# Fused graph-attention layers on one core: layer-0 steps ahead of the W_out products, six summed key tiles in place of five, weights prepared inside entry 0

## Chip, cores and metric

The kernel runs on one core of a Trainium2 chip. Times are device microseconds of that core: the median of ten executions, and one execution recorded by the hardware profiler, from which all durations of single instructions come.

## What is computed

Eight batch entries, each with N = 2048 nodes and D = 256 features, go through two attention layers with residual and layer norm after each. `adj` is one 2048 x 2048 matrix for all entries.

```python
# layer 0, for each of 8 heads of 32 features (the prior is adj itself)
x_proj = einsum('bnd,hdf->bhnf', x, W)
e = leaky_relu(e_src[..., :, None] + e_dst[..., None, :], 0.2)
e = e + softplus(beta_tilde) * log(adj + 1e-6)
attn = softmax(where(adj > 0, e, -max))
x1 = layernorm(x + concat_heads(attn @ x_proj) @ W_out.T)
# layer 1, one head
h1, h2, h3 = x1 @ W1, x1 @ W2, x1 @ W3
p = softmax(where(adj > 0, leaky_relu(h1 @ h2.T, 0.2), -1e12))
out = layernorm(x1 + relu(p @ h3))
```

## The kernel before

**Layer 0** is `Gat`. Its attention weights are products of a query row and a key column under a maximum, times a matrix `mt` that depends on `adj` alone; so a tile of scores for one head and 128 keys, `s`, is one VectorE instruction of 128 x 2048 (L304). Heads are taken in four pairs (NP = 4), keys in sixteen tiles (NT = 16). One *step* is one pair and one key tile: 64 steps per entry. A step loads a 1 MB `mt` tile (L180; two buffers), makes two `s` (four buffers, so two steps' worth), and gives them to TensorE in `products` (L329): `val` multiplies them by the projected features, `den` by the row of key factors `e`, spread over 32 columns, which sums the denominators. Both accumulate in PSUM over the sixteen tiles.

For entries 1 to 7, the key tiles in `SUMMED` don't get `den` products. Instead the first of them is scaled into two tiles `d` by ScalarE (L317), each later one is multiplied and added into `d` by VectorE one step later (L311, one instruction per head), and at the last step one `den<-d,ones` product brings the sums into PSUM.

```python
    SUMMED = (1, 4, 7, 10, 13)
```

`finish` ends a pair: ScalarE copies `val` into `ht` and `den` into `dn`; the denominators go through DRAM (`rc` L346, reciprocal L347, `rec_d` L348) and come back spread over rows as `rb` (L354); after every second pair VectorE multiplies `ht` by `rb` (L356). `rb` takes a buffer of the same two as `d`.

**Between the layers** stands what is called the seam here. `output` (L369) multiplies `ht` by the transposed W_out for sixteen row tiles, giving `y`; VectorE adds the residual (L371) and takes statistics, ScalarE normalizes, the rows go to `x1_d` and stay in `h3`. `turn` transposes them into `x1t` (L384) and multiplies by W3 (L389).

**Layer 1** is `Dot`, sixteen row tiles. `queries` gives `h1` (L409, once for four row tiles), `scores` the products `e` (L420), a mask addition with row minimum on VectorE (L425) and Exp on ScalarE (L426); `step` transposes the result (L439, copied by L441) and multiplies it by `h3` into `acc` (L455).

**The order.** TensorE executes in the order in which the program is written; the instructions of the other engines are put in order by a scheduler when the kernel is built, and each engine, SP's DMA queue among them, then works its list through in order. Entry 0's layer 0 is run first, with the projections of entries 1 to 7 (`project`, six pieces per entry: four row groups, then the exponentials with the multiplication of `v`, then the query rows) spread evenly over its 64 steps, and with `make_pen`, which turns `adj` rows into a bf16 mask in DRAM. During its first pair it also makes the sixteen `mt` tiles (`make_mt`: two passes on VectorE, L165 and L168, two on ScalarE, transposes L173, copies L174). After that, seven times, layer 1 of entry b - 1 runs together with the 64 steps of layer 0 of entry b. The last layer 1 runs alone. The places of the steps are written by hand:

```python
        for k, _ in enumerate(gat.output()):
            if k % 4 == 3:
                layer_0(1)
        for k, _ in enumerate(gat.turn()):
            if k % 2 == 1:
                layer_0(1)
        dot = Dot(gat)
        dot.step(lambda k: layer_0((2, 1, 1)[k]))
        for i in range(NT - 2):
            dot.step(lambda k: layer_0((0, 2 - (i % 2 == 1), 2 - (i % 14 == 13))[k]))
```

That is 4 steps in `output`, 8 in `turn`, 52 in the `Dot` phase. The weights W_out, W1 W2 and W3 are prepared before anything else (L121 to L149): loaded, transposed by TensorE, and W1 W2 multiplied out.

Of the kernel before, what the change touches and what calls it, by code (L numbers as in the profile page):

```python
# [9 lines left out]
F32 = mybir.dt.float32  # L10
BF16 = mybir.dt.bfloat16
I32 = mybir.dt.int32
AF = mybir.ActivationFunctionType
ALU = mybir.AluOpType
# [4 lines left out]
P = 128  # L19
# [4 lines left out]
NO_EDGE = -3.0e38  # L24
# [3 lines left out]
def kernel(  # L28
# [26 lines left out]
    nc = tc.nc  # L55
    B, N, D = x.shape
    H, _, DH = w_proj.shape
    NT = N // P
    KC = D // P
    BK = 512  # L60
    NB = N // BK
    HALF = N // 2
    HP = 2
    NP = H // HP
    IG = BK // P
    SUMMED = (1, 4, 7, 10, 13)

    const = ctx.enter_context(tc.tile_pool(name="const", bufs=1))
    dram = ctx.enter_context(tc.tile_pool(name="dram", bufs=1, space=DRAM))
# [7 lines left out]
    def mm_tile(name):  # L77
        return ps.tile([P, BK], F32, tag="mm", name=name)
# [39 lines left out]
            nc.vector.tensor_mul(wa, wp[:, kc, 0:D], a_bc)  # L118
            nc.vector.tensor_reduce(dst[:, kc, :], wa.rearrange("p (h f) -> p h f", h=H), AX.X, ALU.add)

    def load_square(w, name):  # L121
        t = chunk.tile([P, KC, D], F32, tag="ht", name=name, bufs=3)
        nc.sync.dma_start(t, w.rearrange("(k p) c -> p k c", p=P))
        return t

    def transposed_square(src, dst):
        for kc in range(KC):
            t = mm_tile("sq_t")
            for o in range(KC):
                nc.tensor.transpose(t[:, ts(o, P)], src[:, o, ts(kc, P)], ident)  # L130
            nc.scalar.copy(dst[:, kc, :], t[:, 0:D])


    wot = const.tile([P, KC, D], F32)
    transposed_square(load_square(w_out, "wo"), wot)


    w1t = chunk.tile([P, KC, D], F32, tag="ht", name="w1t", bufs=3)
    transposed_square(load_square(w1, "w1s"), w1t)
    w2t = chunk.tile([P, KC, D], F32, tag="ht", name="w2t", bufs=3)  # L140
    transposed_square(load_square(w2, "w2s"), w2t)
    w12 = const.tile([P, KC, D], F32)
    for dc in range(KC):
        t = mm_tile("w12p")
        for kc in range(KC):
            nc.tensor.matmul(t[:, 0:D], w1t[:, kc, ts(dc, P)], w2t[:, kc, :], start=(kc == 0), stop=(kc == KC - 1))
        nc.scalar.copy(w12[:, dc, :], t[:, 0:D])
    w3s = const.tile([P, KC, D], F32)
    nc.sync.dma_start(w3s, w3.rearrange("(k p) d -> p k d", p=P))  # L149


    mt_d = dram.tile([N, N], F32, name="mt_d")
# [30 lines left out]
    def make_pen(it):  # L183
        a = wide_tile("adj_r", "d", 2, I32)
        nc.sync.dma_start(a, adj[ts(it, P), :])
        pen = wide_tile("pen", "pen", 1, BF16)
        nc.vector.tensor_scalar(pen, a, 0.0, NO_EDGE, ALU.is_le, ALU.mult)
        nc.sync.dma_start(pen_d[ts(it, P), :], pen)

    def layer_norm(z):  # L190
# [16 lines left out]
    class Gat:  # L207
# [8 lines left out]
        def project(self):  # L216


            b = self.b
            kept = "v" if b == 0 else ("h3", "x1t")[b % 2]  # L220
            self.v = v = whole.tile([P, NT, D], F32, tag=kept, name="v")
            ed = small.tile([P, NT, H], F32, name="ed", bufs=1)
            es = small.tile([P, H, NT], F32, name="es", bufs=1)
            xb = x[b].rearrange("(t p) d -> p t d", p=P)
            xrs, xts = [], []

            def turn(g):
                if g % 2 == 0:
                    xr = wide.tile([P, 2 * IG, D], F32, tag="p", name="xr", bufs=2)
                    nc.sync.dma_start(xr, xb[:, ts(g // 2, 2 * IG), :])  # L230
                    xrs.append(xr)
                xt = chunk.tile([P, KC, BK], F32, tag="ht", name="xt", bufs=3)
                for kc in range(KC):
                    t = mm_tile("tr")
                    for k in range(IG):
                        nc.tensor.transpose(t[:, ts(k, P)], xrs[-1][:, g % 2 * IG + k, ts(kc, P)], ident)
                    nc.scalar.copy(xt[:, kc, :], t)
                xts.append(xt)

            turn(0)  # L240
            for g in range(NB):
                if g + 1 < NB:
                    turn(g + 1)
                for k in range(IG):
                    it = g * IG + k
                    t = mm_tile("proj")
                    for kc in range(KC):
                        nc.tensor.matmul(t[:, 0:D + 2 * H], xts[g][:, kc, ts(k, P)], wp[:, kc, :],
                                         start=(kc == 0), stop=(kc == KC - 1))
                    nc.scalar.copy(v[:, it, :], t[:, 0:D])  # L250
                    nc.scalar.copy(ed[:, it, :], t[:, D:D + H])
                    nc.scalar.copy(es[:, :, it], t[:, D + H:D + 2 * H])
                yield
            top = small.tile([P, 2, H], F32, name="top", bufs=1)
            nc.vector.tensor_reduce(top[:, 0, :], ed.rearrange("p t h -> p h t"), AX.X, ALU.max)
            nc.gpsimd.partition_all_reduce(top[:, 1, :], top[:, 0, :], P, bass_isa.ReduceOp.max)
            nc.vector.tensor_tensor(es, es, top[:, 1, :].unsqueeze(2).to_broadcast([P, H, NT]), ALU.add)
            nc.vector.tensor_tensor(ed, ed, top[:, 1:2, :].to_broadcast([P, NT, H]), ALU.subtract)
            self.re = re = small.tile([P, 2, NT, H], F32, name="re", bufs=2)
            nc.scalar.activation(re[:, 0], ed, AF.Exp, scale=-(1.0 - ALPHA))  # L260
            nc.scalar.activation(re[:, 1], ed, AF.Exp)
            v4 = v.rearrange("p t (h f) -> p (t h) f", f=DH)
            nc.vector.tensor_tensor(v4, v4, re[:, 1].rearrange("p t h -> p (t h)").unsqueeze(2).to_broadcast(
                [P, NT * H, DH]), ALU.mult)
            if b > 0:
                nc.sync.dma_start(v_d[b], v)
                nc.sync.dma_start(re_d[b], re)
            yield
            t = mm_tile("est")
            nc.tensor.transpose(t[:, 0:P], es.rearrange("p h t -> p (h t)"), ident)  # L270
            est = row_tile("est")[:, 0:P]
            nc.scalar.activation(est, t[:, 0:P], AF.Exp, scale=1.0 - ALPHA)
            nc.sync.dma_start(c_d[b].rearrange("h (t p) -> (h t) p", p=P), est)
            yield
# [13 lines left out]
        def step(self, count=1):  # L288

            for _ in range(count):  # L290
# [14 lines left out]
                    s.append(sa)  # L305
                v, e = self.v, self.re[:, 1]
                heads = [hp * HP + a for a in range(HP)]
                summed = self.b > 0 and jt in SUMMED
                if self.b > 0 and jt - 1 in SUMMED[1:]:
                    for d, sa, h in zip(self.sums, self.last, heads):  # L310
                        nc.vector.scalar_tensor_tensor(d, sa, e[:, jt - 1, h:h + 1], d, ALU.mult, ALU.add)  # L311
                self.last = s
                self.products(self.val, [v[:, jt, ts(h, DH)] for h in heads], s, jt == 0, jt == NT - 1)
                if self.b > 0 and jt == SUMMED[0]:
                    self.sums = [wide_tile("d", "d", 2) for _ in heads]
                    for d, sa, h in zip(self.sums, s, heads):
                        nc.scalar.activation(d, sa, AF.Copy, scale=e[:, jt, h:h + 1])  # L317
                if not summed:
                    self.products(self.den, [e[:, jt, h:h + 1].to_broadcast([P, DH]) for h in heads], s, jt == 0,
                                  self.b == 0 and jt == NT - 1)  # L320
                if self.b > 0 and jt == NT - 1:
                    self.products(self.den, [ones] * HP, self.sums, False, True)
                if jt == NT - 1:
                    self.finish(hp)
# [143 lines left out]
    gats = [Gat(b) for b in range(B)]  # L468
    for _ in gats[0].project():
        pass  # L470
    others = (1 for g in gats[1:] for _ in g.project())
    pieces = (B - 1) * (NB + 2)
    for k in range(NP * NT):
        gats[0].step()
        for _ in range((k + 1) * pieces // (NP * NT) - k * pieces // (NP * NT)):
            next(others)
        if k >= NT and (k - NT) % 3 == 2:
            make_pen((k - NT) // 3)
    for _ in others:
        pass  # L480


    dot = None
    for b in range(1, B + 1):
        gat, fresh = gats[b - 1], gats[b] if b < B else None

        def layer_0(count):
            if fresh:
                fresh.step(count)

        if fresh:
            fresh.load()
        if dot is not None:
            dot.step()
        for k, _ in enumerate(gat.output()):
            if k % 4 == 3:
                layer_0(1)
        for k, _ in enumerate(gat.turn()):
            if k % 2 == 1:
                layer_0(1)  # L500
        dot = Dot(gat)
        dot.step(lambda k: layer_0((2, 1, 1)[k]))
        for i in range(NT - 2):
            dot.step(lambda k: layer_0((0, 2 - (i % 2 == 1), 2 - (i % 14 == 13))[k]))
    dot.step()


# [29 lines left out]
```

## Time and profile before

| | |
|---|---|
| Median of ten executions | 4519.67 us (4515.73 to 4523.06) |
| Profiled execution, and its span | 4517.64 us, 4515.9 us |
| TensorE products busy | 4307.0 us (95%) |
| TensorE weight loads busy | 2226.0 us (49%) |
| VectorE busy | 3530.6 us (78%) |
| ScalarE busy | 1772.0 us (39%) |
| DMA | 852 MB, 189 GB/s on average |

The span runs from the first to the last recorded instruction. A group of the profile is named by the line of the kernel, the engine, the operation and `out<-in`; then come the count, the busy time, the mean of one instruction in ns, and the idle time of the engine just before these instructions with what ended it. PE is TensorE, PEld its weight loads, DVE VectorE, ACT ScalarE, SPq the queue that issues the DMAs. One fp32 product of the program shows as two in the trace, and products overlap: a `val` or a `den` of one step is 16 products of about 0.6 us each, but the next operation starts 1.7 us later.

### The profile page before, as it was taken

To read this page: it belongs to the slowest core of one execution; us is meant where nothing else is said; L and a number is where in the kernel's file an instruction comes from. 1 tells how busy PE (TensorE), PEld (TensorE's weight loads), DVE (VectorE), ACT (ScalarE), POOL (GpSimd) and SP (SyncE) were. 2 spreads that over 40 slices of the span, in tenths; PEclk is the share of its full clock that TensorE was granted. 3 is DMA by queue.
4 is the path that set the end of the run, shared out by engine and by line. 5 is a ranking of instruction groups with operands and counts; after the bars stand their busy time and mean duration, and the time that the engine had idled before them with its cause. 6 is when DMAs were issued, how large, how long until landed. Compare 5 with 4: busy or idle time off the path is not lost.

```text
span 4515.9 us, 61388 instructions
## 1 busy us (share of the span) xinstructions
PE 4307.0 (95%) x25372; PEld 2226.0 (49%) x25372; DVE 3530.6 (78%) x2541; ACT 1772.0 (39%) x3739; POOL 4.5 (0%) x14
## 2 busy tenths in 40 slices
PE   6888889999999999999999999999999999999899
PEld 4433335445445544555445554555454554555566
DVE  5787788887889888887888888887988888888222
ACT  6622233334333343333433343333333343333554
POOL 0000000000000000000000000000000000000000
PEclk9999999999999999999999999999999999999999
DMA  7788864556555464555545565555545565554211
GB/s 219 261 297 323 299 216 173 193 185 211 186 179 190 159 222 172 193 181 209 190 173 177 181 218 176 187 188 194 209 160 187 179 213 187 182 178 142 68 49 40
DMA packets 252777, 852.06 MB, mean 189 GB/s; under 512 B 33616, under 2 KB 152400, under 8 KB 174928
## 3 DMA queue, kind: packets, MB, share of 16 engines
q1 hardware_dynamic: 252496, 848.13, 53.9%
q8 instruction: 199, 3.26, 0.3%
q14 instruction: 82, 0.67, 0.0%
HBM read 772.15 MB, written 75.37 MB: 188 GB/s over the span
## 4 chain that ended last, share of the span: by engine, by line
PE 65%; DVE 11%; issue 5%; DMA 3%; ACT 1%; SPq 0%; DVEq 0%
PE acc L455 17%; PE e L420 16%; PE val L329 13%; PE den L329 10%; DVE s L304 8%; PE pt L439 5%; DVE d L311 2%; PE y L369 2%; PE h1p L409 2%; DMA mt<-mt_d 1%; DMA rb<-rec_d 1%; ACT p L426 1%; DVE p L425 1%; PE h3p L389 0%; DVE ht L356 0%
## 5 line engine op out<-in xcount | busy, mean ns | idle before, releaser
L304 DVE SCALAR_TENSOR_TENSOR s<-c,re,mt 128x2048 f32<-128x2048 f32 x1024 | 2347.7, 2344 | 247.9 <-PE den L329 176.1
L329 PE MATMUL val<-s,v 128*32 128x512 f32 x8192 | 1040.9, 603 | 74.4 <-DVE s L304 74.2
L455 PE MATMUL acc<-h,pts 128*128 128x256 f32 x4096 | 949.9, 380 | 8.3 <-ACT pts L441 8.3
L420 PE MATMUL e<-x1t,h 128*128 128x512 f32 x2048 | 904.7, 594 | 0.0
L455 PEld LDWEIGHTS acc<-h,pts 128*128 128x128 f32 x4096 | 748.2, 190 | 99.2 <-ACT pts L441 13.3
L329 PE MATMUL den<-s,re 128*32 128x512 f32 x5952 | 751.2, 593 | 0.0
L420 PEld LDWEIGHTS e<-x1t,h 128*128 128x128 f32 x2048 | 379.5, 190 | 450.8 <-issue 421.0
L329 PEld LDWEIGHTS val<-s,v 128*32 128x32 f32 x8192 | 239.0, 110 | 696.3 <-issue 508.9
L441 ACT COPY pts<-pt 128x512 f32<-128x512 f32 x512 | 296.9, 583 | 644.7 <-PE pt L439 644.5
L311 DVE SCALAR_TENSOR_TENSOR d<-s,re,d 128x2048 f32<-128x2048 f32 x224 | 518.4, 2345 | 0.0
L422 ACT ACTIVATE p<-e 128x512 f32<-128x512 f32 x512 | 303.5, 596 | 480.4 <-PE e L420 480.4
L425 DVE CUSTOM_DVE_ANT_0 p<-p,pen 128x2048 f32<-128x2048 f32 x128 | 292.9, 2289 | 251.5 <-ACT p L422 251.5
L329 PEld LDWEIGHTS den<-s,re 128*32 128x32 f32 x5952 | 205.7, 110 | 448.8 <-issue 447.9
L426 ACT ACTIVATE p<-p,neg 128x2048 f32<-128x2048 f32 x128 | 256.8, 2006 | 255.1 <-DVE neg L425 255.1
L439 PEld LDWEIGHTS pt<-ident,p 128*128 128x128 f32 x2048 | 238.1, 141 | 228.4 <-issue 166.4
L439 PE MATMUL pt<-ident,p 128*128 128x128 f32 x2048 | 318.7, 279 | 9.9 <-ACT p L426 9.9
L463 DVE TENSOR_TENSOR z<-z,x1r 128x256 f32<-128x256 f32 x128 | 54.1, 423 | 255.7 <-ACT z L462 251.7
L462 ACT ACTIVATE z<-acc,rec 128x256 f32<-128x256 f32 x128 | 60.6, 474 | 352.6 <-PE acc L455 352.6
L369 PE MATMUL y<-wot,ht 128*128 128x256 f32 x512 | 138.9, 427 | 60.2 <-DVE ht L356 60.1
L197 ACT ACTIVATE f<-mv,eps_ln 128x1 f32<-128x1 f32 x256 | 74.4, 290 | 270.8 <-DVE mv L195 270.7
L369 PEld LDWEIGHTS y<-wot,ht 128*128 128x128 f32 x512 | 106.0, 214 | 100.4 <-DVE ht L356 63.4
L389 PE MATMUL h3p<-w3s,x1t 128*128 128x256 f32 x512 | 132.7, 385 | 6.9 <-ACT x1t L385 6.9
(81 smaller groups left out, 2100.9 us busy)
## 6 DMA issues: line engine op xcount, KB each, us to landing
mt<-mt_d SPq DMA_DIRECT2D x496, 1024.0 KB, 4.8
c<-c_d SPq DMA_DIRECT2D x64, 1024.0 KB, 6.4
pen<-pen_d SPq DMA_DIRECT2D x128, 512.0 KB, 3.3
xr<-in_x_dram SPq DMA_DIRECT2D x16, 1024.0 KB, 8.5
adj_t<-in_adj_dram SPq DMA_DIRECT2D x16, 1024.0 KB, 6.9
mt_d<-mt SPq DMA_DIRECT2D x16, 1024.0 KB, 5.6
adj_r<-in_adj_dram SPq DMA_DIRECT2D x16, 1024.0 KB, 8.1
rb<-rec_d SPq DMA_DIRECT2D x64, 256.0 KB, 4.1
```

Source lines behind the costliest of these rows:

```text
L304: nc.vector.scalar_tensor_tensor(sa, self.cs[a], self.re[:, 0, jt, h:h + 1], mt, ALU.max, ALU.mult)
L311: nc.vector.scalar_tensor_tensor(d, sa, e[:, jt - 1, h:h + 1], d, ALU.mult, ALU.add)
L329: nc.tensor.matmul(dst[ts(q, DH), ts(c, BK)], weights[q % 2], s[q % 2][:, ds(q // 2 * HALF + c * BK, BK)], start=start, stop=stop)
L369: nc.tensor.matmul(y[:, 0:D], ht[:, ts(it, P)], wot[:, g, :], start=(g == 0), stop=(g == 1))
L389: nc.tensor.matmul(t[:, 0:D], x1t[:, kc, ts(it - 1, P)], w3s[:, kc, :], start=(kc == 0), stop=(kc == KC - 1))
L420: nc.tensor.matmul(t, self.h1[:, kc, ts(it % IG, P)], self.x1t[:, kc, ts(c, BK)], start=(kc == 0), stop=(kc == KC - 1))
L422: nc.scalar.activation(p[:, ts(c, BK)], t, AF.Prelu, alpha=ALPHA)
L425: nc.vector.tensor_tensor_reduce(p, p, pen, -1.0, FMAX, ALU.add, ALU.min, neg)
L426: nc.scalar.activation(p, p, AF.Exp, bias=neg, scale=-1.0, accum_out=den)
L439: nc.tensor.transpose(t[:, ts(k, P)], p[:, ts(g * IG + k, P)], ident)
L441: nc.scalar.copy(pt, t)
L455: nc.tensor.matmul(acc, now[:, ts(k, P)], self.h3[:, j, :], start=(j == 0), stop=(j == NT - 1))
```

## The change

Four things change together.

- At a seam, four steps of the next entry's layer 0 are issued ahead of the W_out products. `output` then has two steps in place of four, and the `Dot` phase 50 in place of 52.
- `SUMMED` becomes one list per head pair: tiles 1, 2, 3 and 13 for the first pair, and six tiles for each of the other three.
- The preparation of the weights becomes a generator, run inside entry 0 after its fifth and ninth steps. The projections of the later entries start later and less densely during entry 0's first pair; the last three pieces of entry 7's are done after entry 0's last step, ahead of the four steps of the first seam.
- Smaller ones: the mask is made by ScalarE in two passes in place of VectorE in one, and the two small copies of a projection tile become one.

```diff
-    SUMMED = (1, 4, 7, 10, 13)
+    SUMMED = ((1, 2, 3, 13),) + ((1, 3, 6, 8, 11, 13),) * (NP - 1)
...
-    transposed_square(load_square(w_out, "wo"), wot)
...
+    def later_weights():
...
+        transposed_square(load_square(w_out, "wo"), wot)
+        yield
+        squares = []
+        for w in (w1, w2):
+            squares.append(chunk.tile([P, KC, D], F32, tag="ht", name="sq", bufs=3))
+            transposed_square(load_square(w, "ws"), squares[-1])
+        for dc in range(KC):
+            t = mm_tile("w12p")
+            for kc in range(KC):
+                nc.tensor.matmul(t[:, 0:D], squares[0][:, kc, ts(dc, P)], squares[1][:, kc, :],
+                                 start=(kc == 0), stop=(kc == KC - 1))
+            nc.scalar.copy(w12[:, dc, :], t[:, 0:D])
+        nc.sync.dma_start(w3s, w3.rearrange("(k p) d -> p k d", p=P))
+        yield
...
-        nc.vector.tensor_scalar(pen, a, 0.0, NO_EDGE, ALU.is_le, ALU.mult)
+        nc.scalar.activation(pen, a, AF.Relu, bias=1.0, scale=-1.0)
+        nc.scalar.mul(pen, pen, NO_EDGE)
...
-                    nc.scalar.copy(ed[:, it, :], t[:, D:D + H])
-                    nc.scalar.copy(es[:, :, it], t[:, D + H:D + 2 * H])
+                    nc.scalar.copy(both[:, it, :], t[:, D:D + 2 * H])
...
-                summed = self.b > 0 and jt in SUMMED
-                if self.b > 0 and jt - 1 in SUMMED[1:]:
+                chain = SUMMED[hp] if self.b > 0 else ()
+                if jt - 1 in chain[1:]:
...
-    others = (1 for g in gats[1:] for _ in g.project())
-    pieces = (B - 1) * (NB + 2)
+    others = [(1 for g in gats[1:] for _ in g.project())] + [later_weights()]
+    LEFT = 3
+    pieces, made = (B - 1) * (NB + 2) - LEFT, 0
     for k in range(NP * NT):
         gats[0].step()
-        for _ in range((k + 1) * pieces // (NP * NT) - k * pieces // (NP * NT)):
-            next(others)
+        if k in (4, 8):
+            next(others[1])
+
+        due = max(k - 3, 0) * 2 // 5 if k < NT else 5 + (k + 1 - NT) * (pieces - 5) // (NP * NT - NT)
+        while made < due:
+            next(others[0])
+            made += 1
...
         if dot is not None:
             dot.step()
+        for _ in others[0]:
+            pass
+        layer_0(4)
         for k, _ in enumerate(gat.output()):
-            if k % 4 == 3:
+            if k % 8 == 7:
                 layer_0(1)
...
-            dot.step(lambda k: layer_0((0, 2 - (i % 2 == 1), 2 - (i % 14 == 13))[k]))
+            dot.step(lambda k: layer_0((0, 2 - (i % 2 == 1), 2 - (i % 4 == 3))[k]))
```

## Prediction

> **What bounds the kernel now.** I read three views in this order: the page's groups, the waits of TensorE, and the busy times of the stages with the timelines around a seam. The span is 4515.9 us, the execution took 4517.6, the median of the runs is 4519.7: sums below are made against the profiled one and carried over with those 2 us added.
>
> ```profile
> L304 DVE SCALAR_TENSOR_TENSOR s<-c,re,mt 128x2048 f32<-128x2048 f32 x1024 | 2347.7, 2344 | 247.9 <-PE den L329 176.1
> L329 PE MATMUL den<-s,re 128*32 128x512 f32 x5952 | 751.2, 593 | 0.0
> L311 DVE SCALAR_TENSOR_TENSOR d<-s,re,d 128x2048 f32<-128x2048 f32 x224 | 518.4, 2345 | 0.0
> ```
>
> The first row is one score tile for one head: 2.344 us, two per step, 4.69 us. The third is one addition into a denominator sum, 2.345 us. VectorE's idle time before score tiles is mostly waiting for TensorE to free a buffer, so TensorE leads on average.
>
> ```profile
> PE val L329 <- DVE s L304: 74.2, 52, 10.9
> PE y L369 <- DVE ht L356: 60.1, 8, 19.6
> PE mtp L173 <- DVE m L168: 18.0, 5, 6.6
> ...
> PE sq_t L130 <- DMA w2s<-in_L_gnn_W_dram: 7.4, 1, 7.4
> ```
>
> What TensorE waited for: total, times, longest. The y row is the seams: once 19.6 us, then about 5.4 at each of six seams, then 8.6 at the last.
>
> ```profile
> 209.30:556.80 347.50, 303.22 (x2074) 131.57 (x2070) 273.33 (x140) 79.53 (x320) 3.02 (x6) 0.95 0.85 309
> 556.80:660.30 103.50, 78.55 (x485) 38.02 (x482) 84.18 (x81) 35.54 (x117) 0.00 (x0) 0.90 0.62 217
> 660.30:1092.50 432.20, 430.38 (x2531) 219.00 (x2529) 358.70 (x232) 164.25 (x277) 0.00 (x0) 1.00 0.53 186
> 1092.50:1176.00 83.50, 75.43 (x481) 36.55 (x480) 76.15 (x79) 34.71 (x119) 0.00 (x0) 0.98 0.59 198
> ```
>
> Stages (length, then busy PE, PEld, DVE, ACT): entry 0 after its first head pair; first seam up to the first h1p; Dot phase; second seam. In the Dot phase TensorE is full and VectorE 83%. At the seam VectorE is 91% busy, and TensorE's "busy" includes waiting inside products.
>
> ```profile
> 1088.99 0.35 DVE L347 RECIPROCAL rc<-rc 128x32 f32<-128x32 f32 x1 [3.04 <-DMA rc<-dn]
> ...
> 1096.16 2.29 DVE L356 TENSOR_TENSOR ht<-ht,rb 128x2048 f32<-128x2048 f32 x1 [1.81 <-DMA rb<-rec_d]
> ```
> ```profile
> 1091.63 4.63 SPq L465 DMA_DIRECT2D out_dram<-z  x2
> 1096.30 2.15 SPq L365 DMA_DIRECT2D h<-in_x_dram  x4
> 1098.48 0.66 SPq L180 DMA_DIRECT2D mt<-mt_d  x1
> ```
>
> VectorE's and SP's queues at the second seam: ht is ready at 1098.45, and SP stands behind the last output store until 1096.3.
>
> **What the Trainium skill says.** "Perfetto Trace Analysis", per-engine timelines, calls ACT and DVE "strict FIFO": what stands behind ht in VectorE's queue waits with it. The trace agrees: at 1096.16 the queue idles 1.81 us for rb. The same page, identifying the most-contended engine, calls matmul busy time a poor measure; it agrees, since 75.43 us are called busy in a seam whose products take some 68. "VectorE: DVE Perf Modes", the perf-mode tier table, keeps fp32 operations on two tensors at one element per cycle, 2293 ns at 2048; ours take 2344, so an added sum costs the full price.
>
> **The change, part by part.**
>
> *Sums.* The chains go from 4x5 to 4+3x6 = 22 tiles per entry. One tile's den products take 1.72 us (in the timeline a den starts at 1025.79 and what follows it at 1027.50). TensorE loses 2x1.72 = 3.4 us per entry, 24 over seven entries. Additions go from 32 to 36 per entry, 28x2.345 = +66 us for VectorE.
>
> *Dot phase.* It holds 50 steps in place of 52 (two were moved to the seam). TensorE: two val (3.4), and 36 den in place of 40 (6.9): -10.3 us. VectorE: -9.4 for the two steps, +14.1 for three more pairs of additions, 363 of 422 us. Summed per row block, VectorE needs 31.7 against TensorE's 29.7, 29.6 and 27.9 in three of fifteen blocks; two steps of lead cover most of it, and I take 2 us of stalls per phase (0 to 6).
>
> *A seam, before.* From 1092.5 to the first h1p at 1176.0: 83.5 us, of which TensorE's work is y 14.9, twelve val 20.6, eight den 13.8, turn 18.4 = 67.7; idle 15.8.
>
> *A seam, after.* Products of key tiles 0 to 3 come ahead of y, but tiles 1 to 3 are in the chain, so the cover is 4 val + 1 den = 8.6 us, not 14. Only tiles 0 and 1 can be ready: there are four score buffers. In the built order of VectorE's queue, ht stands ahead of the scores of tiles 2 and 3, and the additions of tile 2 ahead of y's additions. SP loads the mt of tiles 2 and 3 behind the output store, at 1096.3; at 5.2 us to landing (median of the loads around this seam) 1101.5. So: tiles 0 and 1 on TensorE end at 1097.7; scores 2 and 3 run 1101.5 to 1110.8; their val end at 1112.6, the first y follows (1098.5 before). VectorE then: additions of 2 (4.7), eight y rows at 0.83 each as in the trace (6.7), scores of 4 (4.7), additions of 3 (4.7), half of 5, eight rows, other half: 31 us, to 1141.8. Val and den of 5: 3.5. The turn has eight steps with one den left out: 45.4 plus 0.5 for the first x1t, now bound by TensorE. H1p at 1191.3. The seam takes 99 us, +15.8: +6.9 of work moved in, +8.9 idle. If the mt tiles land by 1098.5, +12.8; if each row costs 0.2 more, +19. The moved steps bring their mt loads, v, re, two c and a pair of ACT copies: v, re and c are loaded by 1092.5 as before (v is issued at 1079.6), the mt loads of tiles 0 and 1 too; those of 2 and 3 are the ones priced. The second d buffer is free when ht ends, ACT copies 2.0 us, before scores 3 need it; costs nothing. Over six seams: +95.
>
> *Start.* The weights leave the queue ahead of the projection: the first x transposes stood at 23.2 behind w2s (7.4 us wait). Now the x load is fourth or fifth on SP, issued near 3.3 and landing after 8.5 (its page median): 12. Everything to the first val (60.3) moves up by 11 (8 to 13). The four weight loads (about 0.5 us of SP each) now stand among the adj_t loads, where SP waits for buffers anyway: nothing, or that 2 us.
>
> *First head pair of entry 0.* From 60.3 to 209.3, 149 us, with ten pieces of later projections; steps with a piece took some 12 us, without 7.7. Now four pieces, and two steps with the weights' products (6.6 us of PE): 4x11.5 + 2x10 + 9x8 = 138, with VectorE's floor at 8.2 per step: -11.
>
> *The other three pairs.* Six pieces more (about 5 us of TensorE each, of which I let 20 show), the last three taken out (9 of TensorE, and one v of 4.4 with the wait behind it: -14), pens off VectorE (16x1.22 = 19.5; half counts, VectorE waits for mt in between): -10. Sum -4 (-20 to +12). ACT gets two passes per pen, not in the trace in that form; "ScalarE: Activation LUTs", what ACT_TABLE_LOAD costs, prices any function at 186 + 0.833 ns per element, 1.9 us at 2048, and the trace has Exp at 2.0: 16x4 = 64 us on an engine 23% busy there, hidden by that idle time unless projection copies stand behind it (up to 10, in the range). The 128 saved small copies are 0.19 us each on ACT and count nothing.
>
> *First seam.* Three pieces come first, then v's multiply stands ahead of rc's reciprocal on VectorE, and v_d ahead of rb on SP: ht some 30 us after entry 0's last product in place of 20. With the queue above: 120 against 103.5, +17 (+8 to +22).
>
> *Sum.* -11 -11 -4 +17 +95 + 7x(-10.3+2) = +28. The tail after the last seam has no steps and keeps its 329 us. 4519.7 + 28 = **4548**.
>
> **Rivals.** *The cover works (faster).* At the six seams the idle time does not grow: VectorE hands over scores 2 and 3 and the rows without TensorE noticing, so a seam is longer only by the 6.9 us moved in. For it: y waits 5.4 us now, and the turn is freed of additions. Against it: VectorE's 91% there, with 9.4 us of additions more. Time: 28 - 6x8.9 = -25, 4494. It decides once a seam grows by less than 11.1 (28/6 below 15.8). *A wash:* mt lands in time and no stalls: -18 -14, giving 4516. For it: of SP only one output store stands ahead of the two loads, where two stood; against it: before, tile 2 was loaded at 1073.9 already, now it waits for that store. *VectorE becomes the bound of the Dot phase too:* 8 us of stalls per phase in place of 2: +42, 4590. For it: 363 of 422 us in one strict queue that also waits for z; against: the lead of two steps. *Not doing what it says:* the built queues show the weights' products after the fifth and ninth steps and the three tiles without den, so only its hiding is in doubt.
>
> **How the numbers follow.** Forecast 0.52, cover 0.22, wash 0.14, VectorE bound 0.12. The likeliest alone, with seams +12.8 to +19 (-18 to +19), entry 0 (+-20) and stalls, is 4520 to 4580. Within 0.2% (9 us, about what a measurement of this kernel can tell from no change) lie half of the wash and some of the forecast's lower edge. Faster 0.28 (cover, part of the wash), same 0.13, slower 0.59. Range 4490 to 4583.
>
> **What would show it.** Right: first val near 49; first y of the second seam some 20 us after the Dot phase's last product; no wait at y for ht but waits at val for s; VectorE near 90% in the seam; Dot phases near 424 us. Wrong: seams under 94 us, or Dot phases over 428, or a first h1p after entry 0 outside 630 to 670 (651 expected).

## The result, and the profile after

The changed kernel takes **4584.62 us** (median of 8 runs, 4580.87 to 4589.81) against 4518.93 for the kernel before (28 runs): ratio **1.0144**, 95% interval 1.0135 to 1.0152. It is slower by 65.7 us. The forecast was +28, in a range that ended at 4583. The profiled execution has a span of 4582.8 us against 4515.9, so its stages can be set beside the old ones.

First the groups of the page (busy us and mean ns of one | idle us before them, and what ended most of it):

```profile
L310 DVE SCALAR_TENSOR_TENSOR s<-c,re,mt 128x2048 f32<-128x2048 f32 x1024 | 2352.3, 2345 | 273.6 <-PE den L335 178.3
L335 PE MATMUL den<-s,re 128*32 128x512 f32 x5728 | 730.0, 603 | 1.1 <-ACT dn L349 1.1
L317 DVE SCALAR_TENSOR_TENSOR d<-s,re,d 128x2048 f32<-128x2048 f32 x252 | 583.3, 2344 | 0.3
```

The sums were moved as intended: 224 fewer `den` products in the trace's count, 28 more additions, each at its old price. Now the waits of TensorE (total us, times, longest):

```profile
PE val L335 <- DVE s L310: 166.7, 70, 8.8
PE mtp L177 <- DVE m L172: 25.2, 7, 4.5
...
PE y L375 <- DVE ht L362: 9.5, 1, 9.5
PE sq_t L137 <- DMA ws<-in_L_gnn_W_dram: 5.9, 1, 5.9
```

The wait of `y` for `ht` has gone from 60.1 us to 9.5; the wait of `val` for scores has gone from 74.2 to 166.7. The time that `y` no longer waits came back in front of `val`, and more with it. The last row is a weight that TensorE waits for in the middle of entry 0.

The stages (length, then busy PE, PEld, DVE, ACT, POOL, granted clock, DMA share, GB/s): first head pair of entry 0, first seam, a Dot phase up to the end of its last `acc` product, and the second seam from there to the first `h1p`.

```profile
51.40:217.50 166.10, 127.09 (x854) 67.94 (x854) 121.07 (x62) 97.56 (x136) 0.36 (x1) 0.86 0.69 223
...
579.90:700.20 120.30, 96.80 (x589) 45.55 (x585) 98.35 (x89) 40.17 (x137) 0.36 (x1) 0.90 0.68 235
700.20:1122.30 422.10, 420.54 (x2440) 215.48 (x2438) 359.22 (x232) 164.42 (x277) 0.00 (x0) 1.00 0.52 183
1122.30:1222.30 100.00, 84.75 (x545) 38.51 (x544) 84.82 (x83) 33.03 (x119) 0.00 (x0) 0.93 0.59 201
```

The Dot phase is full of products, as before, and shorter. The pairs of entry 0 and the seams grew, though the first pair holds less TensorE work than before (127.1 us busy in place of 131.1). All stages, in us (the first pair is counted here with its last step, which the prediction's 149.0 left out):

| stage | before | after | difference | forecast |
|---|---|---|---|---|
| start to first `val` | 60.3 | 51.4 | -8.9 | -11 |
| first pair of entry 0 | 155.7 | 166.1 | +10.4 | -11 |
| its other three pairs | 340.8 | 362.4 | +21.6 | -4 |
| first seam, to first `h1p` | 103.5 | 120.3 | +16.8 | +17 |
| second, third seam | 83.3, 84.9 | 100.0, 100.7 | +16.7, +15.8 | +15.8 each |
| a Dot phase | 432.4 | 422.1 | -10.3 | -8.3 |
| last seam and last layer 1 | 325.1 | 326.8 | +1.7 | 0 |

From one first `h1p` to the next it is 522.1 in place of 515.8. The six seams and seven Dot phases together come to about +25 us, where +37 was forecast; entry 0 with the first seam comes to +39.9, where -9 was forecast. Two rows have the wrong sign: the pairs of entry 0.

The second seam's queues, TensorE first (start, length, then what the idle time before ended with):

```profile
1125.72 1.90 PE L335 MATMUL val<-s,v 128*32 128x512 f32 x16
1133.61 1.91 PE L335 MATMUL val<-s,v 128*32 128x512 f32 x2 [5.99 <-DVE s L310]
...
1142.24 2.86 PE L375 MATMUL y<-wot,ht 128*128 128x256 f32 x12
...
1153.33 1.04 PE L335 MATMUL val<-s,v 128*32 128x512 f32 x2 [3.50 <-DVE s L310]
```
```profile
1127.54 2.29 DVE L362 TENSOR_TENSOR ht<-ht,rb 128x2048 f32<-128x2048 f32 x1 [3.56 <-DMA rb<-rec_d]
1131.20 9.14 DVE L310 SCALAR_TENSOR_TENSOR s<-c,re,mt 128x2048 f32<-128x2048 f32 x4 [1.37 <-DMA mt<-mt_d]
1140.26 4.61 DVE L317 SCALAR_TENSOR_TENSOR d<-s,re,d 128x2048 f32<-128x2048 f32 x2
```

This is the queue of the forecast. The last pair of scores that was ready is used up near 1127.6. VectorE then stands at `ht`, waits for the `mt` tile that SP loaded late, and makes four scores in one go; TensorE follows them one by one, and `y` starts at 1142.24, 19.9 us after the Dot phase's last product ended at 1122.3. The additions come next on VectorE, ahead of the rows of `y`, and later TensorE waits again for scores.

### The profile page after: what moved, and what is told of

It is laid out like the page before. It is cut to its first block, busy times and chain, and to the rows that moved or that the text cites. A ratio compares the mean times of both kernels' runs of the same rounds, so it can differ in the third digit from the quotient of the medians.

```text
span 4582.8 us, 60918 instructions
## 1 busy us (share of the span) xinstructions
PE 4320.5 (94%) x25148; PEld 2220.3 (48%) x25148; DVE 3576.5 (78%) x2553; ACT 1811.9 (40%) x3643; POOL 3.8 (0%) x14
## 4 chain that ended last, share of the span: by engine, by line
PE 78%; DVE 7%; ACT 4%; issue 4%; DMA 2%; SPq 0%; DVEq 0%; POOL 0%; POOLq 0%; ACTq 0%
PE e L426 18%; PE acc L461 18%; PE val L335 17%; PE den L335 12%; PE pt L445 5%; DVE s L310 4%; PE h3p L395 3%; PE h1p L415 2%; DMA mt<-mt_d 2%; PE proj L252 1%; DVE d L317 1%; PE tr L390 1%; ACT h L206 1%; ACT p L432 1%; PE y L375 1%
## 5 line engine op out<-in xcount | busy, mean ns | idle before, releaser
L335 PE MATMUL val<-s,v 128*32 128x512 f32 x8192 | 1070.6, 618 | 167.1 <-DVE s L310 166.7
L335 PE MATMUL den<-s,re 128*32 128x512 f32 x5728 | 730.0, 603 | 1.1 <-ACT dn L349 1.1
L317 DVE SCALAR_TENSOR_TENSOR d<-s,re,d 128x2048 f32<-128x2048 f32 x252 | 583.3, 2344 | 0.3
L252 PE MATMUL proj<-wp,xt 128*128 128x272 f32 x512 | 128.5, 403 | 4.3 <-ACT xt L241 2.8
L323 ACT ACTIVATE d<-s,re 128x2048 f32<-128x2048 f32 x56 | 112.0, 2001 | 44.1 <-DVE ht L362 29.2
```

Source lines behind the costliest of these rows:

```text
L335: nc.tensor.matmul(dst[ts(q, DH), ts(c, BK)], weights[q % 2], s[q % 2][:, ds(q // 2 * HALF + c * BK, BK)], start=start, stop=stop)
```

## Experiments on the seam

All kernels below were timed beside runs of the kernel before (medians 4519.3 to 4520.5). A ratio is to that kernel.

**e1_entry0_only** and **e2_seam_only** cut the change in two: e1 has the edits of entry 0 alone (start, weights, pieces, mask, merged copy), e2 the sums and the seam alone.

> Kernel before with the edits of entry 0 alone (weights inside, pieces rescheduled, mask on ScalarE, one copy), sums and seams as before. Theory A (about half of the loss arises in entry 0, as the stage lengths of the two profiles read: start -9, first pair +10, other pairs +22, first seam about +10 for the three pieces put there): 4552, +33 against before. Rival B (entry 0 only looks long because the work was moved into it, and the loss is that of seams and sums): 4519 or less.

> Kernel before with the edits of sums and seams alone, entry 0 as before. Theory A (six seams at +13.5, seven Dot phases at -8.4, first seam about +10): 4550, +32. Rival B (all of the loss is here): 4580 or more.

Measured: e1 4545.47, ratio 1.0057 (1.0042 to 1.0072); e2 4555.16, ratio 1.0076 (1.0060 to 1.0093). That is +25.4 and +35.1, together 60.5 of the 65.7, about half in each as theory A had it: the halves hardly interact. The +37 that the prediction gives the six seams and Dot phases (95 - 58) isn't the same sum as e2's time: in its trace the first `h1p` comes 9.9 us later than before (670.2), which belongs to the first seam's term, and what follows grows by 28. The prediction had the edits of entry 0 make it faster; e1 is slower, its first `h1p` at 686.5 in place of 660.3.

Four more kernels without the edits of entry 0 take the seam apart. `layer_0(n)` is the number of steps ahead of `y`.

```diff
 f1   SUMMED as before;  layer_0(2), then every 8th row;  52 steps in Dot
 f2   SUMMED as before;  layer_0(4), then every 8th row;  50 steps in Dot
 f3   SUMMED of the change;  otherwise as f1
 f4   e2 with  -((1, 2, 3, 13),) + ...   +((5, 8, 11, 13),) + ...
```

> Kernel before with two steps ahead of the W_out products (two left in output, 52 in the Dot phase), sums as before. Theory A (at a seam VectorE's queue is the bound, and what is ahead costs when its scores have to be made between ht and y; two steps are ready and cost nothing): TensorE works 5.2 us while ht is on its way, VectorE's own idle of about 4 us in a seam goes, so -4 per seam, about 4495. Rival B (any step ahead delays y and costs): 4530 or more.

> Kernel before with four steps ahead and 50 in the Dot phase, sums as before. Theory A (scores of tiles 2 and 3 stand between ht and y whatever the sums are): a seam +11, a Dot phase -4, 4550 to 4570. Rival B (it was the additions of tiles 2 and 3 that cost; without them the cover works): 4510 or less.

> Kernel before with two steps ahead, 52 in the Dot phase, and the new sums. Theory A: seam about as before, Dot phase -3, the turn no longer bound by VectorE: 4485 to 4500. Rival B (the additions at the seam cost their full price there): 4520 to 4540.

> Kernel before with four steps ahead, 50 in the Dot phase, the new sums, but the first pair's four tiles 5, 8, 11, 13 in place of 1, 2, 3, 13. Theory A (the 9.4 us of additions at the seam are gone, the scores between ht and y stay, and the turn gets two pairs of additions back): a seam +7 in place of +14, 4515 to 4525. Rival B (the additions were hidden): 4550 to 4560, as with the tiles 1, 2, 3, 13.

| kernel | steps ahead, sums | time | ratio (95%) | Dot phase's last `acc` to `h1p`, second seam |
|---|---|---|---|---|
| before | 0, old | 4519.3 | | 83.3 |
| f1 | 2, old | 4502.59 | 0.9966 (0.9955 to 0.9978) | 82.0 |
| f3 | 2, new | 4499.64 | 0.9960 (0.9948 to 0.9973) | 86.5 |
| f2 | 4, old | 4571.18 | 1.0116 (1.0101 to 1.0131) | 98.3 |
| e2 | 4, new, chain from tile 1 | 4555.16 | 1.0076 (1.0060 to 1.0093) | 100.9 |
| f4 | 4, new, chain from tile 5 | 4508.71 | 0.9976 (0.9967 to 0.9985) | 93.4 |

Theory A came out for f3 and, 8 us high, for f1; f2 lies 1 us above its range, f4 6 us below. Two steps ahead gain 17 to 20 us with either set of sums: that many scores are ready, and in f1 and f3 `y` starts without a wait, 5.2 us after the last `acc`, behind two `val` and one `den`. Two more steps bring the seam 5.2 us of TensorE work (two `val` and one `den` more than in f1 or f3, at 1.72). With f4's sums the seam grows by 6.9 over f3 (86.5 to 93.4), little more than that; in f2 it grows by 16.3 over f1 and in e2 by 14.4 over f3, so some 11 and 9 us of waiting come with it, six times. VectorE in f4, second seam:

```profile
1091.95 2.29 DVE L356 TENSOR_TENSOR ht<-ht,rb 128x2048 f32<-128x2048 f32 x1 [4.45 <-DMA rb<-rec_d]
1095.01 9.14 DVE L304 SCALAR_TENSOR_TENSOR s<-c,re,mt 128x2048 f32<-128x2048 f32 x4 [0.77 <-DMA mt<-mt_d]
1106.78 2.35 DVE L304 SCALAR_TENSOR_TENSOR s<-c,re,mt 128x2048 f32<-128x2048 f32 x1 [2.63 <-DMA mt<-mt_d]
```

The four scores stand behind `ht` as in the changed kernel, but no addition follows them, and VectorE then stands 2.63 us for the next `mt`. From first `y` to `h1p` it is 70.4 us (1108.80 to 1179.22) where e2 needs 79.9 (1113.27 to 1193.18). f4 beats e2 by 46 us by nothing but the choice of summed tiles, more than either theory gave (4515 to 4525 at best). It has two pairs of additions in the seam like e2, but later ones, and tiles 0 to 3 all keep their `den` products, which is cover ahead of `y`. f2 has the second without the first: three `den` ahead of `y` and no addition before the rows of `y`, but seven additions in the seam where f4 has four. It is 4.9 us longer than f4 with one `den` less, so cover alone doesn't do it. The traces of e2 and f4 allow an estimate of the shares. Both seams hold the same products, and f4 has three `den` (5.2 us) ahead of `y` that e2 has behind it. Ahead of `y` f4 takes only 2.0 us longer (23.0 against 21.0), so cover is worth some 3.2; behind `y` it takes 9.5 less, so less waiting is worth some 4.3 beyond the moved work. The seam's length thus follows VectorE's queue, as forecast. Four steps ahead are dear with a chain that begins at tile 1 (e2, f2) and not with the one from tile 5 (f4); with two steps ahead a chain from tile 1 isn't dear (f1, f3).

## Experiments on entry 0

From the changed kernel, one edit at a time:

```diff
 e4   -nc.scalar.activation(pen, a, AF.Relu, ...); nc.scalar.mul(pen, pen, NO_EDGE)
      +nc.vector.tensor_scalar(pen, a, 0.0, NO_EDGE, ALU.is_le, ALU.mult)
 e5   all of later_weights() ahead of the first step (still after entry 0's projection)
 g1   due = (k + 1) * pieces // 64, none left to the first seam
 k1   due = (k + 1) * pieces // 64, three left as in the change
 k2   due as in the change, none left to the first seam
 g2   e5, with no piece in the first pair: all 39 in the other three
```

> Changed kernel with the mask made on VectorE again. Theory A1 (the two ScalarE passes of 2 us stand before the projection copies in ScalarE's queue, and SP's mask stores wait for them): 10 to 20 us faster than the changed kernel, 4565 to 4575. Rival A2 (they are hidden, and the slow part is the projections packed into three pairs): within 6 us of 4585.

> Changed kernel with the weights prepared after entry 0's projection and before its first step. Theory A1 (in the first pair TensorE stands behind the load of a weight square, and VectorE then waits 13.8 us for it in one piece; the first step comes some 7 us later instead): 5 to 12 us faster than the changed kernel, 4573 to 4580. Rival A2 (the first pair is bound by its single free buffer for m, and the hole would have been waited anyway): within 4 us of 4585, or slower by the 7.

> Changed kernel with the projection pieces spread evenly over entry 0's 64 steps as before (none left for the first seam). Theory A2 (packing six more pieces into pairs 2 to 4 costs more there than the first pair gains): 8 to 20 us faster than the changed kernel, 4565 to 4577. Rival A3 (where the pieces stand doesn't matter, TensorE does them anyway, and the first seam's idle time is filled by three of them): 4585 to 4600.

> Run with the weights before the steps (e5), and no projection piece in the first pair at all; all 39 in the other three. To be read from the length of the first pair, 161 us in e5 (first val 54.5, reciprocal 215.7). Theory P (an x tile that waits for its pieces holds one of the two buffers of m, 56 us for the second one in the changed kernel, and makes the chain through VectorE, ScalarE and TensorE serial): 145 us or less, the whole about 4570. Rival Q (the first pair is bound by that chain or by the adjacency loads with or without an x tile): 155 us or more, the whole 4580 or more.

> After, with its 39 pieces spread evenly over all 64 steps, three still left to the first seam. g1_even_pieces (even, none left) took 23.6 us off after. Theory P: the packing costs it (5 pieces in the first pair, 34 to 35 in the other three); then this takes 4558-4568. Theory L3: the three pieces left to the first seam cost it; then this stays at 4578-4587.

> After, packed as it is, but with no piece left to the first seam: 5 pieces in the first pair, 37 in the other three. Theory L3: 4558-4568. Theory P: 4580-4592, since the other three pairs get still more.

Stages from the traces: first `val` to the pair's reciprocal, from there to ScalarE's `ht` copy behind the last `den`, and from there to the first `h1p`. "Pieces" are projection pieces in the first pair / the other three / left to the seam.

| kernel | pieces | first pair | other three | to `h1p` | time | against after |
|---|---|---|---|---|---|---|
| before | 10/32/0 | 159.9 | 334.7 | 105.4 | | |
| after | 4/35/3 | 170.3 | 357.1 | 121.5 | 4584.62 | |
| e4, mask on VectorE | 4/35/3 | 170.2 | 350.4 | 112.9 | 4572.10 | -12.5 |
| e5, weights early | 4/35/3 | 161.2 | 355.6 | 121.8 | 4574.27 | -10.4 |
| k1, spread evenly | 9/30/3 | 169.4 | 330.6 | 118.9 | 4555.60 | -29.0 |
| g1, even, none left | 10/32/0 | 172.4 | 334.8 | 115.4 | 4561.04 | -23.6 |
| k2, packed, none left | 4/38/0 | 172.9 | 349.8 | 121.5 | 4577.30 | -7.3 |
| g2, none in the first pair | 0/39/3 | 152.7 | 350.1 | 117.5 | 4559.15 | -25.5 |

Two traces of the same code don't agree to the last us: in the six kernels that have entry 0 as before (before, e2, f1 to f4) the first pair takes 159.2 to 161.9 us and the other three 332.3 to 338.9. And the intervals below are some 7 us either way, so differences of time under about 8 us aren't clear of noise (k2 against after, g1 against k1).

Ratios to before: e4 1.0117 (1.0102 to 1.0132), e5 1.0121 (1.0106 to 1.0136), k1 1.0078 (1.0061 to 1.0095), g1 1.0093 (1.0077 to 1.0109), k2 1.0128 (1.0113 to 1.0143), g2 1.0087 (1.0066 to 1.0108).

e4 and e5 came out as their first theories had it, and k1 and g1 gained somewhat more. k2 lies between its two theories, nearer to the packing's; g2 lies between its two for the length of the pair.

*The mask* costs 12.5 us on ScalarE, where its two passes take 1.92 and 1.94 us. Waits in those three pairs (total, times, longest), in the changed kernel and then in e4, of SP with the stores of the mask, of VectorE, and of ScalarE with the mask's first pass:

```profile
SPq L193 <- ACT pen L192: 39.7, 8, 10.1
SPq L193 <- ACT both L255: 17.6, 4, 7.3
DVE s L310 <- DMA mt<-mt_d: 53.4, 16, 9.6
DVE s L310 <- PE den L335: 42.6, 14, 5.8
ACT pen L191 <- DMA adj_r<-in_adj_dram: 23.4, 6, 10.7
```
```profile
SPq L192 <- DVE pen L191: 28.7, 9, 11.0
DVE s L309 <- DMA mt<-mt_d: 50.1, 16, 8.8
DVE s L309 <- PE den L334: 24.4, 11, 3.7
```

SP stands at these stores for 57.3 us in place of 28.7, and the loads of `mt` stand behind them in the same queue. But VectorE's wait for `mt` falls by only 3.3 us in e4, and its wait for TensorE to free a score buffer by 18.2. ScalarE, too, stood 23.4 us for the rows of `adj`, with the projection's copies behind it in its queue. That the mask's engine costs 12.5 us is shown; by which of these queues isn't.

*The weights* cost 9.1 us of the first pair; in e5, where they come before it, the first `val` stands 3.1 us later (54.5 for 51.4). Here is the place in the changed kernel, on TensorE and then on VectorE:

```profile
133.19 0.66 PE L137 MATMUL sq_t<-ident,ws 128*128 128x128 f32 x4
139.74 1.09 PE L137 MATMUL sq_t<-ident,ws 128*128 128x128 f32 x4 [5.89 <-DMA ws<-in_L_gnn_W_dram]
141.28 3.54 PE L149 MATMUL w12p<-sq 128*128 128x256 f32 x8 [0.46 <-ACT sq L138]
...
149.21 1.94 PE L177 MATMUL mtp<-ident,m 128*128 128x128 f32 x16
```
```profile
135.15 2.28 DVE L172 SCALAR_TENSOR_TENSOR m<-adj_t,m 128x2048 f32<-128x2048 int32 x1
151.18 1.23 DVE L169 TENSOR_SCALAR m<-adj_t 128x2048 f32<-128x2048 int32 x1 [13.76 <-PE mtp L177]
```

TensorE waits 5.89 us for the load of W2 (the second `ws`), then does weights and, from 144.67, a piece; the transposes of `m` stand behind them. Of the two buffers that `m` uses, a tile of `x` held one (loaded at 122.02, last used after 178), so VectorE waited 13.76 us before it could begin the next `m`.

*The packing* is the largest: k1 takes back 29.0 us. Its first pair holds 9 pieces where the changed kernel's holds 4, and is no longer (169.4 and 170.3). Its other three pairs hold 30 in place of 35 and are 26.5 us shorter. Taking five pieces out of the first pair freed nothing, and the other three pairs are dearer by about 5 us for each of the five that they got. VectorE's wait there for TensorE to free a score buffer, 42.6 us in the changed kernel, is 21.9 in k1; as e4 has 24.4 with the pieces packed, this wait isn't the packing's alone. Leaving three to the seam matters little: with an even spread it is 5.4 us better than leaving none (k1, g1), packed it is 7.3 us worse (k2). The number in the other pairs isn't the whole of it: 35 take 357 us there, but 38 and 39 take 350, a difference hardly above what the same code shows.

Two kernels therefore moved pieces and masks against each other, at the same numbers:

```diff
 h2   masks at (k - NT) % 3 == 0 in place of 2
 h3   due = 5 + ((k + 1 - NT) * 34 + 24) // 48
```

> After, with the mask made at steps 0, 3, 6... of the other three pairs in place of 2, 5, 8...; as many masks and pieces as after. Theory F: where the pieces fall against the masks costs the other three pairs some 14 us (35 pieces take 357 us, while 31.5 take 335 and 39 take 350), so moving one against the other changes that stretch by more than 6 us, to 4565-4578 or to over 4592. Rival N: only the number of pieces and the mask's engine count; the whole stays at 4580-4590.

> After, with the pieces of the other three pairs half a spacing earlier (the first two of them together at the first step); as many as after. Theory F: as for the shifted masks, a change of more than 6 us either way. Rival N: 4580-4590.

Measured: h2 4589.98 (1.0153, 1.0137 to 1.0168), h3 4582.33 (1.0139, 1.0124 to 1.0154). The three pairs took 371.1 and 353.3 us in place of 357.1, but the first `h1p` stood at 703.1 and 703.5, so the seam took up most of the difference: theory F's stretch moved in h2, and the whole didn't. It changed by no more than 5.4 us, as rival N said. The border between these two stages is thus a poor measure; their sum is the better one.

Last, what bounds the first pair when nothing else is in it (g2: 152.7 us, while VectorE's work there is 123)? **h1_third_adj_t** gives g2 a third buffer for the adjacency tiles.

> g2_no_pieces_in_pair0 with every third adjacency tile of the first pair loaded into a buffer that is unused until later (v of the third entry), so three loads can be out in place of two. Theory L: the first pair is bound by the round of its two adj_t buffers (load about 6.2 us to landing, 1.2 on VectorE, 4.0 on ScalarE, 2.3 on VectorE, then the next load may start), so a piece or a weight is dear only where it lengthens that round. With a third buffer the pair falls from 152.7 us (first val to rc's reciprocal) to 136-145, VectorE's own 16 x 8.2 = 131 being the floor, and the whole from 4559 to 4543-4553. Rival W: the pair is bound by the work in it; it stays at 149-153 and the whole at 4555-4563.

VectorE's queue in g2, then in h1, at the same place:

```profile
97.58 1.23 DVE L169 TENSOR_SCALAR m<-adj_t 128x2048 f32<-128x2048 int32 x1
103.91 1.23 DVE L169 TENSOR_SCALAR m<-adj_t 128x2048 f32<-128x2048 int32 x1 [5.09 <-DMA adj_t<-in_adj_dram]
```
```profile
98.55 1.22 DVE L171 TENSOR_SCALAR m<-adj_t 128x2048 f32<-128x2048 int32 x1
103.48 1.23 DVE L171 TENSOR_SCALAR m<-adj_t 128x2048 f32<-128x2048 int32 x1 [3.72 <-PE mtp L179]
```

The wait for the load is gone (19.7 us in the pair, now none), and a wait for the next buffer stands in its place: `m` has only two as well, free once TensorE has transposed them (14.4 us). The pair came to 148.9 us, 3.8 shorter, at the edge of what rival W allowed; the whole was 4569.52 (1.0110, 1.0095 to 1.0125), outside both theories and 10.4 slower than g2: its other three pairs took 353.9 us in place of 350.1 and its first seam 129.8 in place of 117.5, for a reason that wasn't found. This fits a pair bound by the round that an `m` tile makes over SP, VectorE, ScalarE and TensorE with two buffers at each stage. A third buffer for `m` as well would test it, and wasn't run.

**Putting it together.** g3 is f3 with the weights prepared between entry 0's projection and its first step. g4 is the changed kernel with two steps ahead (52 in Dot), the mask on VectorE, the weights ahead of the first step and the pieces spread evenly, three of them left. h4 is g4 with the third adjacency buffer for three tiles.

> Kernel before with two steps ahead, the new sums (f3, 4500), and the weights prepared between entry 0's projection and its first step. Theory A (nothing of the first step needs the weights; first val some 6 us earlier, as 54.5 in e5 against 60.3): 4491 to 4497. Rival (the start is bound by the x and adjacency loads): 4500.

> Changed kernel with two steps ahead and 52 in the Dot phase, mask on VectorE, weights before the steps, pieces even, but the last three still at the first seam. Theory A (what is left of the change in entry 0 is the merged copy, the earlier start and pieces that fill the first seam's idle time): 4480 to 4495. Rival (three pieces at the seam delay rb there by as much as they fill): 4495 to 4510.

> g4_best_b with the third adjacency buffer for three of the first nine tiles of the first pair (v of the third entry needs it afterwards). Theory L: its first pair (164.7 us) loses about 5 to 10 us, the whole 4480-4485. Rival W: 4488-4492.

Measured: g3 4493.70 (0.9942, 0.9925 to 0.9958), **g4 4490.02** (0.9936, 0.9921 to 0.9952), h4 4491.98 (0.9943, 0.9926 to 0.9959). g4 computes all of the reference and beats both kernels, by 29 and 95 us; the three can't be told apart. g3 and g4 lie where their theory A had them, h4 where its rival had it. h4's first pair is 2.4 us shorter than g4's, no more than two traces of the same code differ, and its whole is no better. The merged copy was never taken alone; g3 lacks it and g4 has it, so it can't cost much.

## Why the prediction was wrong

The sign was right, and so was the mechanism of the seam. In the profiled executions entry 0 with its first seam came out 49 us dearer than forecast (+39.9 for -9), and the seams and Dot phases after it 11 us cheaper (+25 for +37): the miss of 38 is what is left of the two.

- **Seams: right.** The second and third seam are 16.7 and 15.8 us longer (15.8 forecast). The signs named beforehand came: `y` hardly waits for `ht`, `val` waits for scores, and the first `y` stood 19.9 us after the Dot phase (some 20). VectorE was 85% busy there, where near 90% was named. Two slips in the sum nearly cancel: its parts for VectorE add to 32.1 us, not 31, and 1191.3 is 15.3 behind 1176.0, not 15.8. The rival "the cover works" put its point at 11.1 us of growth per seam, and the seams lie above it.
- **Dot phase: right but for one term.** It is 10.3 us shorter, which is the TensorE work that was taken out; the 2 us of stalls that the forecast added did not come. "VectorE becomes the bound of the Dot phase" gave 4590, near the measured time, for a cause that isn't there: the Dot phases are full of products and short. A time that fits is not a mechanism that holds.
- **First seam: right in size** (+16.8 for +17), but its cause isn't confirmed. The forecast put it on the three pieces left there and the steps ahead; k2 leaves no piece and has the same 121.5 us, and e4, with only the mask moved back, has 112.9. As time moves over the border of this stage (h2, h3), the match may be luck.
- **Start: nearly** (-8.9 for -11): `x` had landed at 12.6 us.
- **The named sign of being wrong came too:** the first `h1p` after entry 0 stood at 700.2, outside 630 to 670. Two steps of the prediction put it there.
- **"First head pair of entry 0": failed** (+10.4 for -11). The step took "steps with a piece took some 12 us, without 7.7" as the price of a piece (11.5 us for a step with one, 8 without). Steps stay as unequal when no piece is there: the `val` of g2's steps start 5.8 to 13.3 us apart (the last one 3.6). Four pieces cost some 2 us each there (g2 to e5: 8.5 us), and 9 cost no more than 4 (k1); ten cost no more than four either (159.9 us before, 161.2 in e5). So the six taken out freed nothing. And the weights were priced as 4 us of TensorE (two steps of 10 in place of 8), where they cost 9.1: the load that TensorE waits for, and behind it an `m` that can't be freed.
- **"The other three pairs": failed** (+21.6 for -4). The mask was put at -10 for what it freed on VectorE, and ScalarE's 64 us were called hidden by its idle time, with up to 10 us in the range for copies behind them. Moving it back gains 12.5 us. The pieces were put at +6 (20 less 14); spreading them gains 29.

e4, e5 and k1 together gain 52 us when each is done from the changed kernel. Done all together, in g4, they are worth about 39 by estimate: g4 is 94.6 us faster than the changed kernel, and the seam's part of that is about 55.5 (e2 less f3). So the three overlap, and how they share the loss was not settled; nor through which queue the packing and the mask cost what they cost.

## What to carry to other kernels

Before a step is priced by its neighbours (with a piece 12 us, without 7.7), ask what else alternates there: here a stage that goes round pairs of buffers had long and short steps of its own, and work inside it was nearly free while the same work elsewhere was not. That an engine is idle most of the time doesn't show that work moved to it is hidden: ask which loads, stores and copies stand behind that work in order, and price the chain. Ahead of a late operation put just as much work as its inputs are ready for (here two steps), and keep optional work such as extra additions out of the place where their engine is the bound.

## What the runs showed of the hardware

TensorE ran at about half pace after a wait of 4 us in entry 0's first pair. In g2, with and without a wait ahead:

```profile
109.65 3.67 PE L177 MATMUL mtp<-ident,m 128*128 128x128 f32 x16 [4.05 <-DVE m L172]
113.25 2.62 PE L335 MATMUL val<-s,v 128*32 128x512 f32 x16
...
117.53 2.00 PE L177 MATMUL mtp<-ident,m 128*128 128x128 f32 x16
119.45 1.92 PE L335 MATMUL val<-s,v 128*32 128x512 f32 x16
```

After 4.05 us of idle time sixteen transposes take 3.67 us and the `val` behind them 2.62; with no wait ahead they take 2.00 and 1.92. The Trainium skill, "TensorE: Matmul & The Clock Gate", "What's actually happening", says that after an idle window of about 3.4 us the clock falls to half until about as long has been busy. The runs agree: after a shorter wait of 1.77 us, at 80.88, g2's transposes take 2.00. The changed kernel waits at `mtp` seven times, 25.2 us, where the one before waits five times, 18.0, and the granted clock of the first pair is 0.86 against 0.93. The wait shown thus cost itself and some 2.4 us more on TensorE (3.67 and 2.62 against 2.00 and 1.92), which no term of the prediction's sum held; what this added to the pair as a whole wasn't measured.
